# Bringing split operands of attention scores into row layout: DMA from SBUF to SBUF, or through DRAM slots

## The chip, the cores and the metric

The kernel runs on one core of one Trainium2 chip. The metric is the time of one execution in microseconds (us) of device time. The core has five engines that run their own instruction queues in order and wait for each other by semaphores: TensorE (PE; its weight loads are shown as PEld), VectorE (DVE), ScalarE (ACT), GpSimd (POOL) and SyncE (SP), which here only issues DMAs. An instruction at the head of an engine's queue that has to wait holds up everything behind it.

## The reference, cut to what matters

Two layers run one after the other on x of shape (4, 512, 128). The change is in the first layer, whose attention parts are twelve tasks, one for each of four batches in three parts:

```
x = x + 0.5 * ffn(layernorm(x))      # part 0: causal "latent" attention inside, then a mixture of 8 experts
x = x + attn(layernorm(x))           # part 1: full attention
x = x + 0.5 * ffn(layernorm(x))      # part 2: as part 0
# in each part, 16 heads of 8 dimensions:
scores = einsum('bqhd,bkhd->bhqk', q, k) / sqrt(8);  a = softmax(scores);  out = einsum('bhqk,bkhd->bqhd', a, v)
```

The second layer (a chosen-token attention, an additive attention of depth 4, the chosen-token attention again) is not touched.

## The kernel before, in words

**Split operands.** Scores are computed with bf16 operands that together carry f32 precision. q and k (each 128 rows by 512 tokens, f32) are split into three bf16 pieces (`NS` = 3): the leading piece, the leading piece of the remainder, and the rest. A score is the sum over `r` = 0, 1, 2 of products of kA with qA[r]: each of them is a 128-partition tile in which partition 4x + s holds piece s of row x, for four groups of heads (`[P, NG, T]`), and qA[r] pairs the pieces in another rotation. The fourth row of each four (s = 3) is -1 in kA and, in qA[0], half of these rows later hold the (split) maximum of each query's scores, so that the second product comes out as score minus maximum. They must be zero for the first product.

**Making the pieces** (`pieces`, lines 359 to 367): ScalarE writes the leading piece from PSUM (L363), VectorE the remainder (L364, a tile that shares its buffers, tag "v", with the mixture's v of L483), GpSimd the second piece (a cast, L365) and the third (a subtraction, L366). `spread` (L369 to L378) then moves pieces to rows: 12 DMAs of 128 KB from SBUF to SBUF, and from the third task on one more (L374) that sets the maxima's rows of qA[0] back to zero. There are two sets of qA, kA and vA, used by tasks in turn; `fill` (L247) sets the rows that never change, on VectorE, at the start.

**Tasks and units.** `attention` runs a hand-written order over units: a causal task has 10, a full one 16, in all 144, and seven more steps in which only the trailing work runs. In unit n TensorE makes the scores of unit n (`maxima`, L541) with q as the stationary operand, VectorE reduces them to maxima per query and head group, nm (L564 with the causal mask added, L568 without). After a group's last unit, `place_maxima` (L570) is run in the next unit: GpSimd splits the maxima into three pieces (L575 to L578), VectorE transposes them (L580), SP moves them into qA[0] by four DMAs of 4 KB (L584). Some units later (the lag: 5 at the start, 7 from unit 28 on) TensorE makes the scores once more, now transposed and less the maximum (`shifted`, L593), ScalarE takes the exponential (L607), GpSimd masks the diagonal (L613) and TensorE multiplies with the values (L638). PSUM's eight banks are given to products in turn.

**Beside the units** run generators that take one step each half unit: `prepare` of the next task (layernorm statistics on VectorE, the normalised h and, in latent tasks, Y on GpSimd, L330 and L343, transposition and projection on TensorE, the pieces), `place` (which waits until the task two back has left the buffers, then runs `spread` and `values`), `finish`, and the experts' mixture (L274 on TensorE, L479 on ScalarE, L484 on VectorE, L485 on GpSimd), whose gates go through a small DRAM tile (away, L779) and come back broadcast (spread, L470).

**What sets the order.** The program text gives priorities. A scheduler turns it into the order of each engine's instructions by its own model of their times, so an instruction may stand earlier or later in its engine's queue than in the text.

**The start.** Task 0 is prepared ahead of the loop: `fill(0)`, the projections, the pieces, `fill(1)`, constants on GpSimd (L105 to L139 and L259), then `spread`, with its DMAs issued from SP and ScalarE in turn.

Of the kernel before, what the change touches and what calls it, by code (L numbers as in the profile page):

```python
# [8 lines left out]
F32 = mybir.dt.float32  # L9
BF16 = mybir.dt.bfloat16  # L10
AF = mybir.ActivationFunctionType
ALU = mybir.AluOpType
# [30 lines left out]
def tile_macaron(ctx: ExitStack, tc: tile.TileContext, a: dict, out: bass.AP):  # L43
# [52 lines left out]
    causal = const.tile([P, T], F32, name="causal")  # L96
    paired = const.tile([P, P], BF16, name="paired")
    ones = const.tile([P, T], F32, name="ones")
    zeros = const.tile([16, T], BF16, name="zeros")
# [5 lines left out]
    def constants():  # L105


        nc.gpsimd.memset(causal, 0.0)
        make_causal_mask(nc, causal[:, T - P : T], mask_val=NEG)
        nc.gpsimd.memset(ones, 1.0)  # L110
        nc.gpsimd.memset(zeros, 0.0)

    def constants_later():
        nc.gpsimd.tensor_copy(ident_h, ident)
# [119 lines left out]
    def first_layer(opened, picked):  # L234
        with (
# [8 lines left out]
            vAs = [hp.tile([P, NC, NH, 32], F32, name=f"vA{i}") for i in range(2)]  # L244


            def fill(i):  # L247
                for q in qAs[i]:
                    nc.vector.memset(q.rearrange("p g t -> p (g t)").bitcast(F32), 0.0)
                nc.vector.memset(kAs[i], -1.0)  # L250

            fill(0)

            nms = [hp.tile([P, 16], F32, name=f"nm{g}") for g in range(NG)]
            pieces_of = [hp.tile([P, NC, 32], BF16, name=f"mp{g}") for g in range(NG)]
# [27 lines left out]
            class Task:  # L283
# [3 lines left out]
                def __init__(self, part, b, k):  # L287
                    self.part, self.b, self.k = part, b, k
                    self.causal = part != "full"


                    if self.causal:
                        self.units = []
                        for g in range(0, NG, 2):
                            for pieces in ([(g, 3)], [(g, 2), (g, 0)], [(g, 1), (g + 1, 1)], [(g + 1, 2), (g + 1, 0)], [(g + 1, 3)]):
                                at, unit = 0, []
                                for h, c in pieces:
                                    unit.append((h, c, at, (c + 1) * P))
# [6 lines left out]
                    self.qA, self.kA, self.vA = qAs[i], kAs[i], vAs[i]  # L305
                    self.ready = False

                def prepare(self):

                    b = self.b  # L310
                    while self.part == "full" and (0, b) not in mixed:
                        yield
                    h = wp.tile([P, NC, P], F32, name="h")
                    hT = wp.tile([P, T], F32, name="hT", bufs=1)
                    mv = small.tile([P, NC, 2], F32, name="mv")
                    yield from moments_steps(X[:, b], mv)
                    var = mv[:, :, 1]
                    v = small.tile([P, 2 * NC], F32, name="v2")
                    nc.gpsimd.tensor_scalar(v[:, 0:NC], var, 1e-5, None, ALU.add)
                    if self.causal:  # L320


                        nc.gpsimd.tensor_scalar(v[:, NC : 2 * NC], var, 1.0 + 1e-6, 1e-11, ALU.mult, ALU.add)
                    n = 2 * NC if self.causal else NC
                    r = rsqrt(v[:, 0:n], n)
                    yield
                    eng = nc.gpsimd if self.k else nc.vector
                    for c in range(NC):
                        at = n - NC + c
                        eng.tensor_scalar(  # L330
                            h[:, c, :], X[:, b, c, :], mv[:, c, 0:1], r[:, at : at + 1], ALU.subtract, ALU.mult
                        )
                    yield
                    if self.part == "full":
                        nc.gpsimd.tensor_tensor(
                            X[:, b], X[:, b], late["a_bo"].unsqueeze(1).to_broadcast([P, NC, P]), op=ALU.add
                        )
                        nc.scalar.copy(hT, transposed(h))
                        yield
                        wq, wk, self.wv, src = late["a_wq"], late["a_wk"], late["a_wv"], hT  # L340
                    else:
                        for c in range(NC):
                            nc.gpsimd.tensor_scalar(  # L343
                                Y[:, b, c, :], X[:, b, c, :], mv[:, c, 0:1], r[:, c : c + 1], ALU.subtract, ALU.mult
                            )
# [12 lines left out]

                def pieces(self, ps, scale, name):

                    x = [wp.tile([P, T], BF16, name=f"{name}C{s}", bufs=1) for s in range(NS)]
                    rest = wp.tile([P, T], F32, tag="v", name="rest")
                    nc.scalar.activation(x[0], ps, AF.Copy, scale=scale)  # L363
                    nc.vector.scalar_tensor_tensor(rest, ps, scale, x[0], ALU.mult, ALU.subtract)  # L364
                    nc.gpsimd.tensor_copy(x[1], rest)  # L365
                    nc.gpsimd.tensor_tensor(x[2], rest, x[1], op=ALU.subtract)  # L366
                    return x

                def spread(self):  # L369

                    if self.k > 1:
                        nc.sync.dma_start(self.qA[0][NS:P:8], zeros.unsqueeze(1).to_broadcast([16, NG, T]))  # L374
                    moves = [(self.kA[s:P:4], self.kC[s]) for s in range(NS)]
                    moves += [(self.qA[r][s:P:4], self.qC[(s + r) % NS]) for r in range(NS) for s in range(NS)]
                    for i, (to, x) in enumerate(moves):
                        (nc.scalar if self.k == 0 and i % 2 else nc.sync).dma_start(to, x)  # L378

                def values(self):  # L380
                    pv = bank()
# [13 lines left out]
                def place(self):  # L395

                    ago = tasks[self.k - 2] if self.k > 1 else None
                    while not self.ready:
                        yield
                    while ago and now[0] <= ago.start + ago.last[NG - 1] + GAP:  # L400
                        yield
                    self.spread()
                    yield
                    yield
                    while ago and now[0] <= ago.start + len(ago.units) + GAP + LAG:
                        yield
                    self.values()
# [114 lines left out]
            def attention():  # L522
# [47 lines left out]
                def place_maxima(t, g):  # L570

                    m = nms[g].rearrange("p (j c) -> p j c", c=NC)
                    split = pieces_of[g][:, :, 0:16].rearrange("p c (j s) -> p j s c", s=4)
                    rest = wp.tile([P, 4, NC], F32, name="mR")
                    nc.gpsimd.tensor_copy(split[:, :, 0], m)  # L575
                    nc.gpsimd.tensor_tensor(rest, m, split[:, :, 0], op=ALU.subtract)
                    nc.gpsimd.tensor_copy(split[:, :, 1], rest)
                    nc.gpsimd.tensor_tensor(split[:, :, 2], rest, split[:, :, 1], op=ALU.subtract)  # L578
                    mT = wp.tile([P, NC, 32], BF16, name="mT")
                    nc.vector.transpose(mT, pieces_of[g])  # L580
# [828 lines left out]
```

## Time and profile before

| | |
|---|---|
| median of 3 runs | 1445.24 us (1442.93 to 1447.3) |
| the profiled execution: its time, its span | 1445.16 us, 1443.3 us |
| mean granted clock of TensorE | 0.925 |
| DMA, mean over the span | 37 GB/s |

Busy us by stage, from the trace's table of stretches:

| stretch, us | length | PE | DVE | ACT | POOL | PE clock |
|---|---|---|---|---|---|---|
| 0 to 39.5: loads, preparation of task 0 | 39.5 | 7.95 | 14.39 | 4.39 | 32.32 | 0.77 |
| 39.5 to 890: the twelve tasks and the mixtures | 850.5 | 748.68 | 574.95 | 424.02 | 415.38 | 0.91 |
| 890 to 1443: the rest of the mixtures, second layer | 553 | 497.71 | 380.09 | 156.82 | 203.75 | 0.95 |

Products of TensorE overlap, so its busy time is not work at its peak rate; the idle time is what can be read from it. "L541" is line 541 of the kernel. A line of the waits says which instruction was idle, which one released it, for how many us in total, how many times, and the longest. A line of the timeline has the start, the duration, the engine, the line, the operation with what it writes and reads, and in brackets the idle time ahead of it and its releaser. A wait is put down to the last releaser, so behind an in-order engine the instruction named may only have been held up by another one.

### The profile page before, as it was taken

The numbers are of one execution on the slowest core, as the hardware profiler recorded it, in microseconds if no ns is written. First come the engines' busy times: TensorE is split into PE (matmuls) and PEld (weight loads), VectorE is DVE, ScalarE is ACT, GpSimd is POOL, SyncE is SP. The second block draws the span as 40 slices with busy tenths as digits, with TensorE's granted clock in tenths as the row PEclk, the third lists the DMA queues.
The fourth block names the chain that finished last, engine by engine and source line by source line (L and its number), as shares of the span: only waits on it lengthen the run. The fifth ranks groups of instructions, "written<-read, shape, count | busy, mean of one in ns | idle before, by whom it ended". The sixth has DMA issues, their size and how long they took to land. (4 is left out here: it accounts for less than half of the span.)

```text
span 1443.3 us, 32811 instructions
## 1 busy us (share of the span) xinstructions
PE 1254.3 (87%) x12586; PEld 652.5 (45%) x12586; DVE 969.4 (67%) x3321; ACT 585.2 (41%) x1180; POOL 651.5 (45%) x1063
## 2 busy tenths in 40 slices
PE   2787798999998989889769999998969999998698
PEld 0333333343333223334424434346747676766576
DVE  3666676676765767677747754868657676666783
ACT  1244434455555656555425555322313333333122
POOL 8445465666465121214456586561234444443100
PEclk7589799999999999998869999999999999999799
DMA  3201121203012120010103012120100000000000
GB/s 112 71 10 50 37 72 32 77 3 106 4 59 72 35 64 26 25 41 11 49 2 108 26 38 68 39 80 10 29 1 23 16 23 16 1 1 1 1 8 23
DMA packets 66493, 53.07 MB, mean 37 GB/s; under 512 B 24545, under 2 KB 56417, under 8 KB 66337
## 3 DMA queue, kind: packets, MB, share of 16 engines
q1 hardware_dynamic: 63168, 47.86, 11.2%
q10 hardware_dynamic: 3168, 3.12, 0.7%
q8 instruction: 99, 1.62, 0.5%
q14 instruction: 58, 0.47, 0.1%
HBM read 29.45 MB, written 1.18 MB: 21 GB/s over the span
## 5 line engine op out<-in xcount | busy, mean ns | idle before, releaser
L607 ACT ACTIVATE e<-bank 128x512 f32<-128x512 f32 x576 | 312.5, 595 | 303.6 <-PE bank L541 238.7
L541 PE MATMUL bank<-kA,qA 32*128 32x512 bf16 (+3 forms) x2304 | 295.5, 348 | 76.2 <-DVE nm L564 35.4
L564 DVE CUSTOM_DVE_ANT_0 junk<-bank,causal 128x384 f32<-128x384 f32 (+3 forms) x512 | 250.1, 488 | 98.6 <-PE bank L541 58.6
L593 PE MATMUL bank<-qA,kA 32*128 32x512 bf16 (+3 forms) x2304 | 277.8, 342 | 31.7 <-DVE nm L568 17.5
L485 POOL TENSOR_TENSOR hid<-v,spread 128x512 f32<-128x512 f32 x128 | 164.5, 1292 | 96.1 <-DVE v L484 71.2
L638 PE MATMUL sum<-e,vA 128*32 128x256 f32 (+1 forms) x2560 | 195.8, 391 | 9.3 <-POOL e L613 9.3
L593 PEld LDWEIGHTS <-kA 32*128 32x128 bf16 x2304 | 91.1, 95 | 224.3 <-issue 202.7
L568 DVE TENSOR_REDUCE nm<-bank 128x1 f32<-128x512 f32 x256 | 162.5, 682 | 41.2 <-PE bank L541 40.1
L613 POOL TENSOR_SCALAR_AFFINE_SELECT e<-e 128x256 f32<-128x256 f32 x256 | 99.8, 409 | 130.1 <-ACT e L607 129.6
L541 PEld LDWEIGHTS <-qA 32*128 32x128 bf16 x2304 | 105.0, 96 | 95.7 <-issue 82.2
L274 PE MATMUL bank<-tT,sb_f_w 128*32 128x512 f32 x1024 | 140.0, 614 | 2.5 <-DVE v L484 2.3
L274 PE MATMUL sum<-hid,sb_f_w 128*32 128x512 f32 x1024 | 136.0, 598 | 3.0 <-POOL hid L485 2.8
L638 PEld LDWEIGHTS sum<-e,vA 128*32 128x32 f32 x2560 | 65.5, 114 | 142.6 <-issue 125.3
L484 DVE SCALAR_TENSOR_TENSOR v<-th,bank 128x512 f32<-128x512 f32 x128 | 87.4, 684 | 44.9 <-ACT th L479 28.6
L479 ACT ACTIVATE th<-bank 128x512 f32<-128x512 f32 x128 | 76.4, 598 | 54.5 <-PE bank L274 44.3
L156 POOL TENSOR_TENSOR r<-v,mhalf 128x4 f32<-128x4 f32 (+1 forms) x64 | 71.5, 1118 | 5.0
L580 DVE STREAM_TRANSPOSE mT<-mp 128x128 bf16<-128x128 bf16 x48 | 15.0, 312 | 81.2 <-POOL mp L578 80.9
L1283 PE MATMUL bank<-h2T,w 128*128 128x512 f32 x128 | 68.2, 625 | 0.2 <-ACT h2T L1272 0.2
L1289 PE MATMUL bank<-w,hid 128*128 128x128 f32 x512 | 66.9, 280 | 0.1
L1289 PEld LDWEIGHTS bank<-w,hid 128*128 128x128 f32 x512 | 64.0, 197 | 4.5 <-issue 1.0
L1284 ACT ACTIVATE hid<-bank,sb_l_cols 128x512 f32<-128x512 f32 x64 | 44.0, 688 | 39.8 <-PE bank L1283 39.6
L575 POOL CAST mp<-nm 128x16 bf16<-128x16 f32 x48 | 12.3, 256 | 103.2 <-DVE nm L568 74.7
(287 smaller groups left out, 1959.0 us busy)
## 6 DMA issues: line engine op xcount, KB each, us to landing
spread<-away SPq DMA_DIRECT2D x64, 256.0 KB, 3.4
qA<-qC SPq DMA_DIRECT2D x103, 128.0 KB, 2.1
kA<-kC SPq DMA_DIRECT2D x35, 128.0 KB, 2.1
qA<-mT SPq DMA_DIRECT2D x192, 4.0 KB, 1.7
w<-in_l_w_dram SPq DMA_DIRECT2D x8, 256.0 KB, 4.0
sb_m_wqkv<-in_m_wqkv_dram SPq DMA_DIRECT2D x4, 384.0 KB
m_yg<-in_m_trig_dram SPq DMA_DIRECT2D x8, 130.0 KB, 3.2
X<-in_x_dram SPq DMA_DIRECT2D x4, 256.0 KB
```

Source lines behind the costliest of these rows:

```text
L274: nc.tensor.matmul(ps[32 * j : 32 * j + 32, :], lhsT=w[:, 32 * j : 32 * j + 32], rhs=rhs, start=start, stop=stop, skip_group_check=True,)
L479: nc.scalar.activation(th, ph, AF.Tanh, scale=0.5)
L484: nc.vector.scalar_tensor_tensor(v, th, 1.0, ph, ALU.add, ALU.mult)
L485: nc.gpsimd.tensor_tensor(hid, v, self.spread[e], op=ALU.mult)
L541: nc.tensor.matmul(ps[:, at : at + w], lhsT=t.qA[r][rows, g, c * P : (c + 1) * P], rhs=t.kA[rows, g, 0:w], start=r == 0 and k == 0, stop=r ...
L564: nc.vector.tensor_tensor_reduce(junk[:, 0:w], src, causal[:, T - w : T], 1.0, NEG, ALU.add, ALU.max, dst)
L568: nc.vector.tensor_reduce(dst, src, axis=AX.X, op=ALU.max)
L593: nc.tensor.matmul(ps[:, at : at + w], lhsT=t.kA[rows, g, kc * P : (kc + 1) * P], rhs=t.qA[r][rows, g, q0:T], start=r == 0 and k == 0, sto ...
L607: nc.scalar.activation(es[n][:, j, :], ps, AF.Exp)
L613: nc.gpsimd.affine_select(out=e, in_=e, pattern=[[0, 2], [1, P]], compare_op=ALU.is_ge, fill=0.0, base=0, channel_multiplier=-1,)
L638: nc.tensor.matmul(to[32 * j : 32 * j + 32, q0 + lo - at : q0 + hi - at], lhsT=t.vA[:, kc, 4 * j + g, :], rhs=es[n][:, j, lo:hi], start=fresh,
L1289: nc.tensor.matmul(pm[:, c * P : (c + 1) * P], lhsT=hid[:, f, c * P : (c + 1) * P], rhs=w2[:, f, :], start=(f == 0), stop=(f == 3),)
```

## The change

The lines of the changed kernel are given as it has them.

- q and k are split in two steps. `leading` makes the first piece (ScalarE) and the remainder (VectorE, in a buffer of its own, one each for q and k in turn); one half unit later `trailing` makes the other two. For the first task they are VectorE's (a copy L386 and a subtraction L387); for all others the cast is ScalarE's (L383) and the subtraction GpSimd's (L384).
- From the second task on the pieces go through DRAM. `away` writes them to slots, each 128 rows of 1 KB (four DMAs: 384, 256, 128 and 384 KB); `back` reads kA and each of the three qA in one DMA of 512 KB, in which each partition takes 4 KB from the slot of its piece. Slots with zeros and with -1 are written once (`fixed_rows`), so that the rows of the maxima come back as zeros with the rest. Two sets of slots are used in turn. The clearing DMA of L374 and the filling of the second set of buffers are gone.
- The first task keeps moves from SBUF to SBUF (`first_rows`), with the pieces rotated the other way.
- `place_maxima` only splits; the transposition and the DMAs (`move_maxima`) are put on the list of the next unit.
- The causal mask is kept in bf16. The zeros of 16 rows that GpSimd set are gone; VectorE sets a tile of zeros and one of -1 at the start.

```diff
-            def fill(i):
-                for q in qAs[i]:
-                    nc.vector.memset(q.rearrange("p g t -> p (g t)").bitcast(F32), 0.0)
-                nc.vector.memset(kAs[i], -1.0)
-
-            fill(0)
+            for q in qAs[0]:
+                nc.vector.memset(q.rearrange("p g t -> p (g t)").bitcast(F32), 0.0)
+            nc.vector.memset(kAs[0], -1.0)
+            zeros = wp.tile([P, 2 * T], BF16, tag="aT", bufs=1, name="zeros")[:, 0:T]
+            nc.vector.memset(zeros.bitcast(F32), 0.0)
+            minus = wp.tile([P, 2 * T], BF16, tag="junk", bufs=1, name="minus")[:, 0:T]
+            nc.vector.memset(minus, -1.0)
+            qds = [dp.tile([10, P, T], BF16, name=f"qd{i}", bufs=1) for i in range(2)]
+            kds = [dp.tile([NS + 1, P, T], BF16, name=f"kd{i}", bufs=1) for i in range(2)]
+            def fixed_rows():
+                for i in range(2):
+                    nc.sync.dma_start(qds[i][9], zeros)
+                    nc.sync.dma_start(kds[i][NS], minus)
...
-                    self.qC = self.pieces(ps, HD**-0.5, "q")
+                    self.qC, rest = self.leading(ps, HD**-0.5, "q")
+                    yield
+                    self.trailing(self.qC, rest)
+                    yield
                     yield
                     ps = bank()
                     by_columns(ps, wk, src)
-                    self.kC = self.pieces(ps, 1.0, "k")
+                    self.kC, rest = self.leading(ps, 1.0, "k")
+                    yield
+                    self.trailing(self.kC, rest)
                     self.ready = True
...
+                def leading(self, ps, scale, name):
+                    x = wp.tile([P, NS, T], BF16, name=f"{name}C", bufs=1)
+                    rest = wp.tile([P, T], F32, name="rest", bufs=1)
+                    nc.scalar.activation(x[:, 0], ps, AF.Copy, scale=scale)
+                    nc.vector.scalar_tensor_tensor(rest, ps, scale, x[:, 0], ALU.mult, ALU.subtract)
+                    return x, rest
+                def trailing(self, x, rest):
+                    if self.k:
+                        nc.scalar.copy(x[:, 1], rest)
+                        nc.gpsimd.tensor_tensor(x[:, 2], rest, x[:, 1], op=ALU.subtract)
+                    else:
+                        nc.vector.tensor_copy(x[:, 1], rest)
+                        nc.vector.tensor_tensor(x[:, 2], rest, x[:, 1], ALU.subtract)
...
+                def away(self):
+                    def put(slots, x):
+                        nc.sync.dma_start(slots.rearrange("s p t -> p s t"), x)
+                    put(self.qd[6:9], self.qC)
+                    put(self.qd[0:6:3], self.qC[:, 1:3])
+                    put(self.qd[5:6], self.qC[:, 0:1])
+                    put(self.kd[0:NS], self.kC)
+                def back(self):
+                    def rows(slots):
+                        return slots.rearrange("s (x g) t -> x s g t", g=NG)
+                    nc.sync.dma_start(self.kA, rows(self.kd))
+                    for r in range(NS):
+                        nc.sync.dma_start(self.qA[r], rows(self.qd[(6, 3, 0)[r] : 10 : r + 1]))
...
                     while not self.ready:
                         yield
+                    yield
+                    self.away()
+                    yield
                     while ago and now[0] <= ago.start + ago.last[NG - 1] + GAP:
                         yield
-                    self.spread()
+                    self.back()
...
                     nc.gpsimd.tensor_tensor(split[:, :, 2], rest, split[:, :, 1], op=ALU.subtract)
+                    later.append(lambda: move_maxima(t, g))
+                def move_maxima(t, g):
                     mT = wp.tile([P, NC, 32], BF16, name="mT")
                     nc.vector.transpose(mT, pieces_of[g])
...
-            fill(1)
...
-            tasks[0].spread()
+            tasks[0].first_rows()
+            fixed_rows()
```

More of the change, by code (lines that the diff above doesn't have):

```diff
@@ L95, in tile_macaron @@
     ident_h = const.tile([P, P], BF16, name="ident_h")
-    causal = const.tile([P, T], F32, name="causal")
+    causal = const.tile([P, T], BF16, name="causal")
     paired = const.tile([P, P], BF16, name="paired")
     ones = const.tile([P, T], F32, name="ones")
-    zeros = const.tile([16, T], BF16, name="zeros")
     before = const.tile([P, NE, NE], F32, name="before")
@@ L110, in constants @@
         nc.gpsimd.memset(ones, 1.0)
-        nc.gpsimd.memset(zeros, 0.0)
     def constants_later():
@@ L305, in __init__ @@
                     self.qA, self.kA, self.vA = qAs[i], kAs[i], vAs[i]
+                    self.qd, self.kd = qds[i], kds[i]
                     self.ready = False
@@ L355, in prepare @@
                     by_columns(ps, wk, src)
-                    self.kC = self.pieces(ps, 1.0, "k")
+                    self.kC, rest = self.leading(ps, 1.0, "k")
+                    yield
+                    self.trailing(self.kC, rest)
                     self.ready = True
[L359 to L376, printed above, removed]
-                    for i, (to, x) in enumerate(moves):
-                        (nc.scalar if self.k == 0 and i % 2 else nc.sync).dma_start(to, x)
+                def leading(self, ps, scale, name):
[4 more added lines that the diff above has]
+                    return x, rest
@@ new lines, in trailing, with first_rows @@
+                def trailing(self, x, rest):
[5 more added lines that the diff above has]
+                        nc.vector.tensor_tensor(x[:, 2], rest, x[:, 1], ALU.subtract)
+                def first_rows(self):
+                    moves = [(self.kA[s:P:4], self.kC[:, s]) for s in range(NS)]
+                    moves += [(self.qA[r][s:P:4], self.qC[:, (s - r) % NS]) for r in range(NS) for s in range(NS)]
+                    for i, (to, x) in enumerate(moves):
+                        (nc.scalar if i % 2 else nc.sync).dma_start(to, x)
```

## The prediction

> **What bounds the kernel now.** The page's busy shares come first: TensorE 87%, VectorE 67%, ScalarE 41%, GpSimd 45%. TensorE is the engine to keep fed, and the stretch tables say where it is not. From 0 to 39.5 us it is busy 7.95 us; from 39.5 to 890 us (first layer) 748.7 of 850.5 us; after that 497.7 of 553 us. The change touches the first two stretches only, so the list of waits is read for them. Its columns are the waiting instruction, what released it, total us, times, longest.
>
> ```profile
> PE bank L541 <- DMA kA<-kC: 21.8, 1, 21.8
> DVE mT L580 <- POOL mp L578: 80.9, 45, 10.1
> PE bank L541 <- DVE nm L564: 35.4, 23, 7.4
> PE bank L593 <- DVE nm L568: 17.5, 3, 7.9
> ```
>
> The reader is to see one long wait (TensorE on the first task's kA) and one repeated chain: the transposition of the maxima waits for GpSimd, VectorE's reductions wait behind it, and TensorE waits for their banks. The timeline at the start (start, duration, engine, line) shows who makes kA late:
>
> ```profile
> 16.57 0.66 DVE L364 SCALAR_TENSOR_TENSOR rest<-bank,kC 128x512 f32<-128x512 f32 x1
> ...
> 34.80 0.61 POOL L365 CAST kC<-rest 128x512 bf16<-128x512 f32 x1
> 35.40 0.81 POOL L330 TENSOR_SCALAR h<-X,mv,r 128x128 f32<-128x128 f32 x1
> 36.18 1.15 POOL L366 TENSOR_TENSOR kC<-rest,kC 128x512 bf16<-128x512 f32 x1
> 37.32 2.35 POOL L330 TENSOR_SCALAR h<-X,mv,r 128x128 f32<-128x128 f32 x3
> ...
> 39.56 3.48 PE L541 MATMUL bank<-kA,qA 32*128 32x512 bf16 x38 [21.76 <-DMA kA<-kC]
> 39.66 3.14 POOL L343 TENSOR_SCALAR Y<-X,mv,r 128x128 f32<-128x128 f32 x4
> ...
> 52.67 0.25 POOL L575 CAST mp<-nm 128x16 bf16<-128x16 f32 x1 [9.88 <-DVE nm L564]
> ...
> 53.94 0.31 DVE L580 STREAM_TRANSPOSE mT<-mp 128x128 bf16<-128x128 bf16 x1 [0.87 <-POOL mp L578]
> ```
>
> VectorE has the remainder of k at 17.2, but GpSimd, full of constants and the preparation of tasks 1 and 2, splits it only at 37.3. Kernel start, then, hangs on GpSimd's queue.
>
> **Step 1, first task's split on VectorE.** Added to VectorE's start: memsets of zeros (a quarter of the 0.91 us row) and minus (a quarter of the 1.76 us row), with gaps 1.1 us; removed from it: the second filling, 3 x 0.91 + 1.76 us, which lay beside waits. All that hangs on the first statistics moves 1.1 us later. ScalarE's copy of q then ends at 15.9 (14.15 + 0.60 + 1.1). VectorE follows with remainder 0.66, copy, subtraction, for q and k. The trace has no such copy; nearest are a VectorE operation with one f32 SBUF input at 0.55 us (L985) and a copy out of PSUM at 0.68 (L959). I take 0.55. The subtraction is as the two-input rows, 0.66. Two times 1.9 us and small gaps: kC complete at 19.7. From GpSimd's last split to the first product it was 39.56 - 37.33 = 2.2 us; so the first product comes at 21.9, 17.6 us earlier.
>
> It doesn't all arrive. Group 0 of the first task took 52.67 - 39.56 = 13.1 us, set by VectorE's reductions, so its maxima would be done at 35.0. The next step is GpSimd's split of them, and in the built order of the changed kernel GpSimd still has the preparation of tasks 1 and 2 ahead of it. That run ended at 42.80 and had no gap after 9.6; it loses four operations (0.62 + 1.15 + 0.61 + 1.15 = 3.53) and the memset of zeros (0.52), and starts 1.1 later: 39.85. The split takes 1.27, so the transposition comes at 41.1 instead of 53.94: **12.8 us gained**, with the gate handed from kA to GpSimd's backlog. Bounds: 17.6 if the backlog isn't in the way. If GpSimd's traffic slows the four new VectorE operations by 1.0 us each (one two-input row, L722, took 1.70 instead of 0.66), the maxima are done at 39.0, still under the 39.85.
>
> [...] In the trace L722's eight runs are 0.66 us but for one of 1.70, which started during a GpSimd multiplication. [...]
>
> **Step 2, maxima split one unit ahead.** If it worked as worded, the repeated chain would go. I read the order of instructions in both built programs: the scheduler places them, and in it the transposition stands where it stood, right behind the last reduction of its group (47 of 48 within four VectorE instructions), with GpSimd's h and Y ahead of the split as before. The six longest stalls of TensorE that follow a transposition (7.44 at 146.9, 2.20 at 182.1, 5.53 at 256.0, 7.85 at 470.2, 4.80 at 534.9, 4.80 at 600.0) have the same sequence of work ahead of them. Taken: 0. Bounds: 0 to 32.6 gained, the sum of the six.
>
> One place changes for the worse: ahead of the stall at 470 the two statistics that start h and Y stand four reductions later than before (behind 12 and 14 of a group's 16, not 8 and 10). Reductions come in pairs every 1.45 us, so GpSimd's 14 us chain starts **2.9 us** later against the group's end. Bounds 0 to 2.9.
>
> **Step 3, remainders.** k's remainder now stands later than right behind the transposition. TensorE's waits for remainders (L364) are 6.9 + 5.5 + 1.9 = 14.3 us in this stretch; the bank then waited for is that of the next reduction, 0.55 us instead of 0.69, behind the same transposition. I take **3 us gained**; bounds 0 and 14.3. For tasks 1 to 11 the cast goes from GpSimd (0.61) to ScalarE (0.60 by its f32-to-bf16 row L363), 22 times. GpSimd gains little: it waited 41.0 us for these remainders. ScalarE's cast waits for VectorE, and exponentials queue behind it: 0.8 us in the usual case (the remainder ends at most 0.83 after ScalarE's copy in 14 of the 22, up to 3.4 in the others) plus 0.60. Taken: 0, since ScalarE waits 238.7 us for L541's banks and already carries copies of 0.59 us between exponentials; bounds 0 and 22 x 1.4 = 31 us lost.
>
> **Step 4, DRAM slots.** Per task 13 issues of SP (12 moves of 128 KB, one of 64 KB) become 8: 1.15 MB out in four, 2 MB back in four. Issue is 0.6 us each; landing is 2.3 us for 256 KB out (out_dram), 3.4 to 4.0 us for 256 KB in (spread, w). No row shows 512 KB alone; the load phase moved 244 to 339 GB/s, so 2 MB take 6 to 8.5 us and some 3 us to land. The old moves took 8 us and 2.1: no later. Both wait for the same last product two tasks back; three units remain, some 16 us (850.5 us over 151 units are 5.6 each). The maxima's small moves queue behind them, but at lag 7 have four units. Two tight places: task 4, whose k is split after its predecessor's third group (out and back end at about 289 in before's time, needed at 289.7), and group 1 of the first task (57 to 58, needed at 57.3). I take **1 us lost**; bounds 0 and 3 us at each of 11 tasks, 33. The nearest row for a short way out and back is away, 16 KB: issued at 173.06, its first reader at 174.55. [...]
>
> **Step 5, causal in bf16.** A 512-wide reduction takes 0.686 us with the mask and 0.682 without: nothing to gain, 0.
>
> **Sum**: -12.8 + 0 + 2.9 - 3 + 0 + 1 + 0 = -11.9 us. The profiled execution took 1445.16 us (span 1443.3 and 1.9 around it), the median is 1445.24: **1433 us**.
>
> **Rivals.** (a) The transposition does stop waiting: up to 32.6 us more, 1401. For it: the program text; against it: the built order. (b) The change doesn't do what it says on time: the first 12.8 us are given back in changed stalls (three or four more shifts like the 2.9 us of step 2, since every statistic in the built order has moved a little), 1441 to 1449. (c) **Slower**: ScalarE's casts block it. Each of 22 holds exponentials 1.4 us; banks go back late and TensorE stops. Full price 31 us: 1433 + 31 = 1464. It decides from 16.2 / 22 = 0.74 us paid per cast (the sum reaches +0.3%, 4.3 us). For it: ScalarE is in order, two exponentials (1.09 us) fill most of a 1.45 us half unit in the full attention; against it: only 2.6 us of TensorE's waits in this kernel are on a ScalarE copy (oU, 7 times, longest 0.6).
>
> **Numbers.** Forecast 1424 to 1441: 0.62. Beyond it, (a) in part or whole or the full 17.6 us: 0.13. (b) 0.12. (c), with late read-backs, 0.13. What a measurement of this kernel can tell from no change is 0.3%, so faster means below 1440.9: 0.75; the same 0.12; slower 0.13. The range leaves out most of (a) and of (c): 1417 to 1447.
>
> **What would show it.** First product near 22; first transposition near 41 with some 5 us of wait on GpSimd's mp; 75 to 85 us on that wait in all; the 7 to 10 us stalls of the first and second part still there; no TensorE wait on kA or qA above 1 us later than the start; ScalarE waits for rest near 18 us, with TensorE's waits on ScalarE under 8. A first product after 28, a short mT wait in total, or TensorE waiting on qds or kds would prove me wrong.

## The result, and the profile after

The changed kernel is slower: 1459.47 us median (1455.5 to 1461.17, 4 runs) against 1444.09 us (1442.02 to 1447.3), a ratio of 1.0101 with a 95% interval of 1.0071 to 1.0131. The forecast was 1433 us. The profiled execution has a span of 1459.0 us and a clock of 0.92; the time went in the second stage, the first layer: from 39.5 to 890 us TensorE is busy for 733.70 us, not 748.68.

The start did what was forecast. The timeline of the changed kernel:

```profile
15.02 3.54 POOL L270 MEMSET vA<- 128x2048 f32 x2
...
16.32 3.54 DVE L386 CAST qC<-rest 128x512 bf16<-128x512 f32 x1
...
21.41 0.52 DVE L386 CAST kC<-rest 128x512 bf16<-128x512 f32 x1
...
25.16 1.03 PE L583 MATMUL bank<-kA,qA 32*128 32x512 bf16 x9 [7.37 <-DMA kA<-kC]
...
40.35 0.25 POOL L617 CAST mp<-nm 128x16 bf16<-128x16 f32 x1
...
41.61 0.31 DVE L625 STREAM_TRANSPOSE mT<-mp 128x128 bf16<-128x128 bf16 x1 [1.55 <-POOL mp L620]
```

The first product comes at 25.16, not 39.56, the first transposition at 41.61, not 53.94: 12.33 us gained. To see where they went again, line up the 48 transpositions of the two kernels, one for each group of each task, and follow the difference (the expectations below call this the ledger). It is -12.3 us at the first, still -10.5 as the fifth task begins (318.5 before), +3.7 two groups later, +11.4 at the third group of the sixth task, and +11 to +18 from there on. So some 28 us were lost, and the difference made 22 of them in three groups.

Such a step says that a group ended later, not that TensorE stood still for it. In the last of the three (8.3 us) TensorE's stall is 4.1 us longer than before (11.91 against 7.85); the trace also has 32 more of the mixtures' products between these two transpositions than before, work that had only moved. Nor is idle time the whole loss: against the kernel with the first task's split alone (the first experiment; span 1430.4 us), the changed kernel's span is 28.6 us longer with the same 12586 products. TensorE's idle time grew by 16.3 us (176.2 to 192.5) and its busy time by 12.3 (1254.2 to 1266.5). The last section shows what may be one reason for the second: behind each stall of over 4 us in this stage the granted clock was 0.50 for some us, and behind the one near 470 a pair of products took 0.60 to 0.63 us, not 0.38 or 0.39.

The waits of the first 890 us (waiting instruction, releaser, total us, times, longest):

```profile
DVE mT L625 <- POOL mp L620: 102.6, 45, 12.4
...
PE bank L583 <- DVE nm L606: 25.5, 22, 5.5
PE bank L638 <- DVE nm L610: 23.5, 6, 11.9
...
ACT kC L383 <- DVE rest L377: 20.9, 10, 10.6
...
PE bank L638 <- DVE rest L377: 11.9, 6, 8.8
PE bank L583 <- ACT e L652: 10.9, 14, 1.5
...
PE bank L583 <- DMA kA<-kC: 7.4, 1, 7.4
```

Against before: the transposition's wait for GpSimd did not go but grew (80.9 to 102.6). One row is new: TensorE behind exponentials, 14 times some 0.8 us. And the waits of the second product behind a remainder (before 5.5 us, 2.6 at most) now hold one of 8.8 us. That one is the group with the first large loss. Read its timeline from the bottom up:

```profile
318.63 3.52 SPq L403 DMA_DIRECT2D qd<-qC  x3
...
322.28 0.48 SPq L824 DMA_DIRECT2D away<-gT  x1
...
324.81 1.62 SPq L417 DMA_DIRECT2D qA<-qd  x2
...
326.54 1.95 SPq L512 DMA_DIRECT2D spread<-away  x4
...
333.68 1.26 POOL L527 TENSOR_TENSOR hid<-v,spread 128x512 f32<-128x512 f32 x1 [12.10 <-DMA spread<-away]
...
336.14 0.31 DVE L625 STREAM_TRANSPOSE mT<-mp 128x128 bf16<-128x128 bf16 x1 [10.23 <-POOL mp L620]
...
337.06 0.62 ACT L383 CAST kC<-rest 128x512 bf16<-128x512 f32 x1 [10.57 <-DVE rest L377]
337.08 0.58 PE L638 MATMUL bank<-qA,kA 32*128 32x512 bf16 x1 [8.75 <-DVE rest L377]
```

The gates leave at 322.28. Behind them on SP's queue stand two read-backs of the slots, which hold SP until 326.4; only then go the gates' broadcast loads, and these land 7 us later, behind 1 MB of read-back. GpSimd, whose next instruction needs them, stood 12.10 us. In the kernel before it was 2.26 at this place:

```profile
331.43 1.27 POOL L485 TENSOR_TENSOR hid<-v,spread 128x512 f32<-128x512 f32 x1 [2.26 <-DMA spread<-away]
```

The maxima's split stands behind it on GpSimd, the transposition behind that, k's remainder behind the transposition on VectorE, the cast behind the remainder on ScalarE, and TensorE behind all of them.

### The profile page after: what moved, and what is told of

Read it like the earlier page. It is cut to its first block, busy times and chain, and to the rows that moved or that the text cites. A ratio compares the mean times of both kernels' runs of the same rounds, so it can differ in the third digit from the quotient of the medians.

```text
span 1459.0 us, 32733 instructions
## 1 busy us (share of the span) xinstructions
PE 1266.5 (87%) x12586; PEld 655.4 (45%) x12586; DVE 972.1 (67%) x3323; ACT 596.5 (41%) x1202; POOL 632.4 (43%) x1036
## 5 line engine op out<-in xcount | busy, mean ns | idle before, releaser
L638 PE MATMUL bank<-qA,kA 32*128 32x512 bf16 (+3 forms) x2304 | 281.5, 347 | 55.4 <-DVE nm L610 23.5
L683 PE MATMUL sum<-e,vA 128*32 128x256 f32 (+1 forms) x2560 | 194.7, 388 | 10.5 <-POOL e L658 8.6
L638 PEld LDWEIGHTS <-kA 32*128 32x128 bf16 x2304 | 93.1, 96 | 233.7 <-issue 207.7
L281 PE MATMUL bank<-tT,sb_f_w 128*32 128x512 f32 x1024 | 144.6, 620 | 3.1 <-DVE v L526 2.3
L625 DVE STREAM_TRANSPOSE mT<-mp 128x128 bf16<-128x128 bf16 x48 | 14.9, 310 | 102.9 <-POOL mp L620 102.6
L1226 PE MATMUL bank<-wa,hT 128*128 128x385 f32 x128 | 56.7, 543 | 1.4 <-ACT hT L1219 1.4
```

Of the source, the lines that this page charges most:

```text
L281: nc.tensor.matmul(ps[32 * j : 32 * j + 32, :], lhsT=w[:, 32 * j : 32 * j + 32], rhs=rhs, start=start, stop=stop, skip_group_check=True,)
L638: nc.tensor.matmul(ps[:, at : at + w], lhsT=t.kA[rows, g, kc * P : (kc + 1) * P], rhs=t.qA[r][rows, g, q0:T], start=r == 0 and k == 0, sto ...
L683: nc.tensor.matmul(to[32 * j : 32 * j + 32, q0 + lo - at : q0 + hi - at], lhsT=t.vA[:, kc, 4 * j + g, :], rhs=es[n][:, j, lo:hi], start=fresh,
```

## The experiments

First theory: the slots' transfers hold up urgent small ones. Their DMAs are called puts (`away`, to DRAM) and read-backs (`back`). Rivals: ScalarE's casts block it; the added pauses (the new `yield`s, each half a unit long) shift the order of the work. The change has these three parts besides the first task's split, and all eight combinations were run. Each time is compared with the kernel before on the same chip (1444.2 to 1445.4 us in the five sets).

**The first task's split alone**, in the kernel before:

```diff
-                    nc.gpsimd.tensor_copy(x[1], rest)
-                    nc.gpsimd.tensor_tensor(x[2], rest, x[1], op=ALU.subtract)
+                    eng = nc.gpsimd if self.k else nc.vector
+                    eng.tensor_copy(x[1], rest)
+                    eng.tensor_tensor(x[2], rest, x[1], op=ALU.subtract)
```

> The kernel before with one edit: the first task's two later pieces of q and k are made on VectorE, not on GpSimd. In the changed kernel the first transposition began 12.33 us earlier than before, and the ledger of the 48 transpositions stands 27 us worse at 700 us. If those 27 us belong to other parts of the change, the 12.3 us stay: 1432 us. If the later stretches give back whatever the start gains, 1440 to 1444.

Measured: 1431.02 us, ratio 0.9905 (0.9887 to 0.9923). The 12.3 us of the first transposition are there at every later one (9.7 to 13.4). Nothing gives them back; the loss belongs to the other parts.

**One part undone each time.** The slots, with the moves from SBUF to SBUF in their place (the main lines):

```diff
-                    put(self.qd[6:9], self.qC)
...
-                    nc.sync.dma_start(self.kA, rows(self.kd))
+                    moves = [(self.kA[s:P:4], self.kC[:, s]) for s in range(NS)]
+                    moves += [(self.qA[r][s:P:4], self.qC[:, (s - r) % NS]) for r in range(NS) for s in range(NS)]
+                    for to, x in moves:
+                        nc.sync.dma_start(to, x)
```

> The changed kernel with the twelve moves from SBUF to SBUF in the place of the slots (the read-back's place), all else as changed. Theory of the slots: the puts and read-backs on SP's queue hold up the gates' broadcast loads (12.10 us of wait at 333.7, where the gates had left at 322.3), and the two steps of 6.35 and 7.89 us in the fifth task go with them: 1445. Theory of the casts on ScalarE, and theory of the shifted steps of the preparation: within 3 us of the changed kernel, 1457 to 1462.

Measured: 1442.84 us, 0.9991 (0.9975 to 1.0008): 16.6 us less than the changed kernel. The rows of zeros come from a small DRAM tile, and the second set of buffers is filled by VectorE as before. The casts, back on GpSimd:

```diff
-                        nc.scalar.copy(x[:, 1], rest)
+                        nc.gpsimd.tensor_copy(x[:, 1], rest)
```

> The changed kernel with the 22 casts of the second piece back on GpSimd, nothing else. Theory of the casts: the 14 half-unit stalls of TensorE behind ScalarE, 10.9 us in all, go, and the 11.9 us that TensorE stood behind the remainder go in part: 1446 to 1449. Theory of the slots and of the shifted steps: 1456 to 1462, as GpSimd gets 22 casts of about 0.6 us more.

Measured: 1447.22 us, 1.0009 (0.9994 to 1.0025): 12.3 less. TensorE's waits behind exponentials fall from 10.9 to 1.2 us on the first product; GpSimd's wait for the gates' loads at 330 is still there, 12.39 us. The maxima's two steps, in one again:

```diff
-                    later.append(lambda: move_maxima(t, g))
-                def move_maxima(t, g):
```

> The changed kernel with the maxima's splitting and transposition in one step again. VectorE's built order differs in one transposition of 48, GpSimd's and ScalarE's not at all; on SP the moves of the transposed maxima change places with the gates' loads. All three theories: 1456 to 1462; a gain of over 5 us would say that the places on SP's queue decide and that the split of the step is what moved them.

Measured: 1455.57 us, 1.0068 (1.005 to 1.0087), lower than the range written down, but the interval overlaps that of the changed kernel: not told apart. Of this part there is nothing large to find. The pauses, taken out:

```diff
                     self.qC, rest = self.leading(ps, HD**-0.5, "q")
-                    yield
                     self.trailing(self.qC, rest)
-                    yield
                     yield
...
                     self.kC, rest = self.leading(ps, 1.0, "k")
-                    yield
                     self.trailing(self.kC, rest)
...
-                    yield
                     self.away()
-                    yield
```

> The changed kernel with the added pauses of the preparation and of the placing taken out again: remainder's split in the same step as its product, k in the step after q, puts and read-back without pauses between; slots and ScalarE's casts stay. Theory that the shifted steps cost: where the slots and the casts were undone, the fifth and sixth task's third groups still fell back by 7.7 and 8.3 us, so these go: 1443 to 1449. Theory that slots (16.6) and casts (12.3) make up the whole loss: 1456 to 1462.

Measured: 1441.87 us, 0.9966 (0.9951 to 0.9981): 17.6 less. Three parts that seem to cost 16.6, 12.3 and 17.6 us cannot all do so: the whole loss against the split alone is 28. So the parts were also run alone, with the same edits combined. Pauses alone:

> The changed kernel without slots and with the casts on GpSimd; the added pauses stay. If the two prices add: 1459.5 - 16.6 - 12.3 = 1430.6. If both sat in one stall (the 10.23 us at 336): 1440 to 1443.

Measured: 1433.95 us, 0.9918 (0.9894 to 0.9943). None of the three:

> Without slots, casts on GpSimd, without the added pauses: of the change only the first task's split on VectorE, the remainder's own buffer, the maxima's two steps and the bf16 mask are left. As the first task's split alone, if those three are worth nothing: 1428 to 1434. If the remainder's own buffer brings something, below 1425.

Measured: 1432.87 us, 0.9923 (0.9902 to 0.9943): as the split alone. Own remainder buffer, bf16 mask and the maxima's two steps are worth nothing that can be measured. Slots alone:

> As the kernel with nothing left but the first task's split, yet with the slots in DRAM: casts on GpSimd, no added pauses. If the slots cost by themselves, as in the pair that left them out (16.6): 1444 to 1449. If they cost only where the pauses bring their transfers ahead of the gates' loads: 1429 to 1435.

Measured: 1432.09 us, 0.9916 (0.9895 to 0.9937). The slots alone cost nothing, and my first theory as I had put it falls. Casts alone:

> As the kernel with nothing left but the first task's split (1432.9), yet with the 22 casts on ScalarE; no slots, no added pauses. If the casts cost by themselves, as in the pair that differs in them beside the slots (1441.9 against 1432.1): 1441 to 1445. If, like slots and pauses, they cost only in company: 1431 to 1435.

Measured: 1444.01 us, 0.9991 (0.9978 to 1.0004). All together, medians in us:

| | slots: no | slots: yes |
|---|---|---|
| no casts on ScalarE, no pauses | 1432.9 | 1432.1 |
| pauses | 1434.0 | 1447.2 |
| casts | 1444.0 | 1441.9 |
| casts and pauses | 1442.8 | 1459.5 |

The casts cost 9 to 12 us in every company. Slots and pauses cost nothing singly (-0.8 and +1.1) and 14 together. For the pauses that nothing is a balance: in the profiles, the transposition of the fifth task's second group comes 21.7 us earlier than in the kernel before with pauses alone, and 11.8 with none of the three; the last transposition, 11.9 and 11.8. Two questions follow: why together, and by what the casts cost.

**Why slots and pauses together.** With the pauses q is ready before the gates of the task three back, so the scheduler puts q's puts and read-backs ahead of the gates' loads on SP; without them the loads come first. Only that order is changed here, in the kernel with slots and pauses (1447.2):

```diff
-                    self.back()
+                    if self.k == 5:
+                        while not loads_of:
+                            yield
+                        with tc.issue_after(loads_of[0]):
+                            self.back()
+                    else:
+                        self.back()
```

> The changed kernel with the casts on GpSimd (1447.2) and one more edit: the sixth task's read-backs are put on SP's queue behind the first four of the gates' loads, which they stand among or ahead of. On every other engine the built order is the same, on SP two read-backs move. If the loads' place behind the read-backs makes the 11 us wait for the maxima near 333: the wait falls to about 4, and 1440 to 1442. If it is the amount that the slots move, whatever the order: 1446 to 1449.

Measured: 1443.07 us, 0.9982 (0.9967 to 0.9997), 4.1 less. The place, for comparison with the one above:

```profile
320.65 0.34 SPq L830 DMA_DIRECT2D away<-gT  x1
...
322.97 1.95 SPq L518 DMA_DIRECT2D spread<-away  x4
...
325.04 1.24 SPq L417 DMA_DIRECT2D qA<-qd  x2
...
326.32 1.26 POOL L533 TENSOR_TENSOR hid<-v,spread 128x512 f32<-128x512 f32 x1 [6.51 <-DMA spread<-away]
```

Loads first, and GpSimd waits 6.51, not 12.39. The amount moved is the same. The other losses of this pair are at 109 and 172. Of the first, the DMA table of the changed kernel from 95 to 112 us shows the reason (KB each, median us from issue to landing):

```profile
qA<-qd SPq DMA_DIRECT2D x3, 512.0 KB, 8.0
...
qA<-mT SPq DMA_DIRECT2D x4, 4.0 KB, 7.0
```

Moves of 4 KB that land in 1.8 us by the median of the whole run took 7.0 here, issued behind three of 512 KB. TensorE stood 3.07 us for one. Both places were put in order as well:

```diff
+                    elif self.k == 2:
+                        while (1, 1) not in sent:
+                            yield
+                        with tc.issue_after(sent[1, 1]):
+                            self.back()
...
+                    if self.k == 3 and 0 in sent:
+                        with tc.issue_after(sent[0]):
+                            put(self.kd[0:NS], self.kC)
...
+                    while self.k == 3 and 0 not in sent:
+                        yield
```

> The kernel with the sixth task's read-backs behind the gates' loads (1443.1), and two more such moves on SP's queue: the third task's read-backs behind the moves of the second task's second group of maxima, where TensorE stood 2.66 us for such a move at 108.7; and the fourth task's put of k behind the first gates' loads. VectorE, GpSimd and ScalarE keep their built order. If the order on SP's queue is the whole price of slots and pauses together: 2.7 there, and some 5 at 172 where the maxima waited 5.70 us and not 1.7: 1434 to 1437. If the amount moved is: 1441 to 1445.

Measured: 1437.42 us, 0.9942 (0.9925 to 0.9958). Three changes of order on one queue, with the orders of VectorE, GpSimd and ScalarE untouched, take 9.8 of the 13.3 us by which slots and pauses (1447.2) stood above pauses alone (1434.0). The last 3.4 us lie within the intervals; whether anything is left there is open. The amount moved was the same in these three kernels, so it is not the amount that made these 9.8.

**By what the casts cost.** Each cast takes 618 ns, and ScalarE waits for its remainder first. One experiment adds the work without the wait:

```diff
+                        nc.scalar.copy(x[:, 2], x[:, 0])
                         nc.gpsimd.tensor_copy(x[:, 1], rest)
```

> The kernel with nothing left but the first task's split (1432.9, casts on GpSimd), and 22 copies on ScalarE of the size of the casts, each right behind the activation that made its source, so that it waits for nothing; what they write is overwritten by the third piece. The casts on ScalarE cost 11 us. If what costs is ScalarE's 0.6 us of work: 1442 to 1445. If it is ScalarE's standing still for VectorE's remainder: 1432 to 1435.

Measured: 1433.54 us, 0.9927 (0.9907 to 0.9947). 22 copies of 618 ns each cost nothing. The other keeps the casts (no slots, pauses; 1442.8) and takes the wait away:

```diff
-                        nc.scalar.copy(x[:, 1], rest)
+                        with tc.issue_after(last_exp[0]) if last_exp[0] else ExitStack():
+                            nc.scalar.copy(x[:, 1], rest)
```

> The kernel without slots (added pauses, casts on ScalarE; 1442.8), with each cast put behind the two exponentials that come next in ScalarE's queue; there it stood right behind the activation of the first piece, and waited 26 us in all for VectorE's remainder. VectorE's order hardly changes. If the price of the casts (8.9 us against the same kernel with them on GpSimd, 1434.0) is that wait: ScalarE's waits for the remainder fall below 10 us, the stalls of TensorE behind exponentials go, and 1434 to 1437. If it is the work: 1441 to 1445.

Measured: 1432.16 us, 0.9916 (0.9899 to 0.9932): the whole price is gone. The waits with the casts right behind their activation, 40 to 890 us:

```profile
ACT kC L377 <- DVE rest L371: 13.2, 10, 4.0
ACT qC L377 <- DVE rest L371: 13.2, 11, 3.0
...
PE bank L571 <- ACT e L640: 11.0, 14, 1.5
```

and with the casts two exponentials later:

```profile
ACT qC L378 <- DVE rest L371: 3.3, 2, 1.7
ACT kC L378 <- DVE rest L371: 3.2, 3, 2.8
...
PE bank L572 <- ACT e L641: 1.5, 1, 1.5
```

ScalarE's 26.4 us of waiting became 6.5, and TensorE's 11.0 behind exponentials 1.5. So the wait is the price, by these two runs; the way from it to TensorE is shown only in part. With the casts alone (no pauses) the same row has 4.8 us, against 0.4 in the kernel with none of the three, for the same price of 11. And in the profiles of either pair TensorE's idle time differs by 4.1 us; the rest stands in its busy time, in products that took longer (7.5 and 9.6 us). What made them longer there was not found.

**The stall near 470.** The pauses put the statistics of the next two preparations later; GpSimd's chain behind them sets the transposition. First the kernel with slots alone, then the changed one:

```profile
436.29 0.23 POOL L327 TENSOR_SCALAR v<-mv 128x4 f32<-128x4 f32 x1 [9.90 <-DVE mv L171]
...
452.07 0.31 DVE L620 STREAM_TRANSPOSE mT<-mp 128x128 bf16<-128x128 bf16 x1 [9.36 <-POOL mp L615]
...
453.01 0.61 PE L633 MATMUL bank<-qA,kA 32*128 32x512 bf16 x2 [7.85 <-DVE nm L605]
```

```profile
464.93 0.23 POOL L327 TENSOR_SCALAR v<-mv 128x4 f32<-128x4 f32 x1 [12.21 <-DVE mv L171]
...
480.63 0.31 DVE L625 STREAM_TRANSPOSE mT<-mp 128x128 bf16<-128x128 bf16 x1 [12.39 <-POOL mp L620]
...
481.57 0.61 PE L638 MATMUL bank<-qA,kA 32*128 32x512 bf16 x2 [11.91 <-DVE nm L610]
```

From v to the transposition it is 15.8 and 15.7 us in both: GpSimd's r, h, X, r, h and Y stand ahead of the split of the maxima. The stall grew by 4.1 us. With pauses alone it is 11.98, so the slots and the casts have no part in it. Since the chain is GpSimd's, part of it was moved, in the kernel with slots alone:

```diff
-                            nc.gpsimd.tensor_scalar(
+                            nc.vector.tensor_scalar(
                                 Y[:, b, c, :], X[:, b, c, :], mv[:, c, 0:1], r[:, c : c + 1], ALU.subtract, ALU.mult
```

> The kernel with the slots alone (casts on GpSimd, no added pauses; 1432.1), and the normalized rows Y (20 instructions, 797 ns each on GpSimd) on VectorE. GpSimd's backlog ahead of the maxima at 450, 15.7 us long, gets 3.1 shorter, others of latent tasks as well: 1426 to 1430 if the backlog is what the stalls hang on. If VectorE's own time decides: 20 x 386 ns = 8 us more there, 1434 to 1440.

Measured: 1421.07 us, 0.9832 (0.9818 to 0.9847), the fastest of all, 11 us under the same kernel with Y on GpSimd. TensorE's stall at this place:

```profile
446.30 1.16 DVE L351 TENSOR_SCALAR Y<-X,mv,r 128x128 f32<-128x128 f32 x4 [5.32 <-POOL r L154]
...
448.12 0.58 PE L633 MATMUL bank<-qA,kA 32*128 32x512 bf16 x1 [5.56 <-DVE nm L605]
```

It is 5.56, not 7.85, and now VectorE stands for r in the middle of its reductions; the four rows of Y take 1.16 us there and took 3.14 on GpSimd. The transposition's waits for GpSimd fall to 51.8 us in all (78.8 with Y on GpSimd). Between 100 and 890 us TensorE's stalls of over 4 us are four, 26.3 us in all, and not six of 38.4. Four more tried how far this goes: h on VectorE too (`eng = nc.vector`), the second piece's casts on VectorE too, Y on VectorE with pauses and without slots, and Y on VectorE with neither.

> As the one with Y on VectorE, and h there too (44 more instructions in the part up to 890 us). If GpSimd's backlog decides: the 7.85 us stall at 453 goes nearly whole and the two of 4.80 in part: 1418 to 1426. If VectorE, which would stand behind the root r on GpSimd (1.0 to 1.7 us each time, more behind a backlog), is blocked instead: 1436 or more.

Measured: 1430.53 us, 0.9898 (0.9882 to 0.9913), a miss. VectorE stands 24.0 us in 9 waits of h for r. Against Y alone 4.7 us are lost by the second group of the sixth task; what takes them there was not followed further.

> The kernel with Y on VectorE (1421.1), and the casts of the second piece on VectorE too: 22 x 0.62 = 13.6 us less for GpSimd, and no hand-over between remainder and cast; VectorE gets 22 x 0.52 = 11 us more (the first task's second cast). If GpSimd's backlog still sets the stalls: 1414 to 1419. If VectorE is now as late as GpSimd: 1421 to 1427.

Measured: 1425.57 us, 0.987 (0.985 to 0.989): no gain over Y alone, a loss of 4.5.

> The kernel without slots, with the added pauses and the casts on GpSimd (1434.0), and Y on VectorE. If Y's place brings what it brought beside the slots (11.0): 1423. If the remainder stalls that the pauses remove (3.3 and 3.5 us, still there with Y on VectorE) come on top: 1416 to 1420.

Measured: 1423.02 us, 0.9849 (0.983 to 0.9868): Y brings 10.9 us without slots and with the pauses as well; the remainder stalls do not come on top.

> The fastest kernel so far (slots, no added pauses, casts on GpSimd, Y on VectorE; 1421.1) with moves from SBUF to SBUF in the place of the slots. If the slots bring nothing by themselves, as without Y's move (1432.1 against 1432.9): 1419 to 1424. If they bring something once GpSimd is less late: 1425 or more.

Measured: 1427.98 us, 0.9894 (0.9874 to 0.9914): 7 us above the kernel with slots, against the first of the two expectations. They are there from the start: VectorE fills the second set of buffers (0.91, 0.91 and 1.76 us) ahead of q's remainder, the first transposition is at 45.89 and not 43.15, the second task's second group at 107.95 and not 101.59. With slots that filling isn't needed.

## Why the prediction was wrong

- **Step 1** (first task on VectorE, -12.8): right, -12.33 at the first transposition, and -14.0 us alone between the medians of the first experiment's set. GpSimd's backlog set the moment (split at 40.35, forecast 39.85). The first product came at 25.16, not at 21.9, near the 25.9 of the bound with four operations slowed by 1.0 us each (21.9 + 4.0); it was one cast that took 3.54 us, so the nearness is luck. The backlog covered it, as forecast, but by 0.3 us and not by 4.9 (39.85 less 35.0): VectorE had the last maximum at 40.06. The wait on mp was 1.55, not 5, for this reason.
- **Step 2** (maxima, 0; statistics near 470, +2.9): right in kind. The transposition's waits grew, the stalls stayed, and the stall at 470 grew by 4.1. Rival (a) is refuted: 102.6 us of wait. The cause was put down to the split of the maxima; the runs show that it is the pauses, as it is 7.85 or 7.86 in the kernels without them (before, slots alone, none of the three, slots and casts).
- **Step 3, remainders** (-3): with the pauses, without slots and casts, TensorE's waits for remainders are 8.2 us, without any of the three 14.2: a gain of about 6 that does not reach the time (pauses alone: +1.1). The longer stall at 470 takes back 4.1 of it; the rest was not followed.
- **Step 3, casts** (0; GpSimd's waits for the remainders were 41.0 us for q alone and 47.3 with k's, and nothing hangs on it): this term was mis-sized; it is 9 to 12 us, 0.5 us a cast. Rival (c) had its mechanism, and the reason for setting it to nothing was the error: that ScalarE has 238.7 us of idle time and carries copies of 0.59 us already. That is true of its work, and the copies without a wait cost nothing. But the price of an instruction in an in-order queue that waits for another engine is not its work. Alone it brings the time from 1432.9 to 1444.0, no change from before; rival (c)'s 31 us were too much, and its row, TensorE behind exponentials, shows only a part of the price.
- **Step 4** (slots, +1): alone right (-0.8), but 14.3 us with the pauses of step 3. Beside the casts, this is the step that failed, at its words "no later": it asked when kA and qA arrive, and TensorE hardly ever waited for those (0.3 us after the start). It did not ask who stands behind the puts and read-backs on SP: the gates' loads and the maxima's moves. Its words "the maxima's small moves queue behind them, but at lag 7 have four units" miss the start, where the lag is 5 and a move took 7.0 us. The built order showed both; I had read VectorE's and GpSimd's order and not SP's.
- **The sum**: the steps were priced one by one and added. Two of them had one price together that neither had alone; the built order of the whole change is where it could be seen. No step asked for the granted clock behind a stall (0.50). Rival (b), gains given back because the order moved, named the kind; its 8 to 16 us were too few.
- **Step 5** (mask, 0): no run disagrees; it is part of the 1432.9.

## What to carry to other kernels

When a change moves transfers, read the order on the issuing queue as closely as that of the compute engines, and ask of each large transfer which small, urgent one stands behind it: here 10 us hung on three places in SP's order. Price an instruction that is moved to a less busy engine by what it waits for, not by its length: 22 copies without a wait cost nothing, 22 with one cost 9 to 12 us, and two exponentials' distance made them free again. And where a repeated wait names one engine, look what else that engine does just ahead of it: thirty-two small instructions taken off GpSimd brought 11 us, to 1421 us, about as much as the first task's split.

## What the runs showed of the hardware

The first task's cast of q took 3.54 us on VectorE and that of k, of the same shape, 0.52. Beside the first, GpSimd ran six memsets without a gap, the two of 128x2048 from 15.02 to 18.56 and four small ones to 19.57; the cast ended at 19.86, 0.29 us after them. In the kernel with Y on VectorE and no slots, where the casts (at 20.75 and 22.87) came after these memsets (done at 16.45), both took 0.40. So the cast beside the memsets was 7 times as long as its fellow; that the memsets held it up is the author's estimate from these rows, and by what way they would no run shows.

A small transfer's time to landing depended on what stood ahead of it on the same queue: 4 KB took 1.8 us by the median and 7.0 behind three of 512 KB, and 1.8 by the median at that place (90 to 112 us) in the kernel with all three places in order; a gates' load of 256 KB took 3.0 us at best and 7.2 behind read-backs. It was not always paid for: the load of 7.2 us was issued at 779.51, and GpSimd's last wait for such a load in the first 890 us ended at 776.59. Whether another queue would have let the small ones pass was not tried.

The granted clock fell at TensorE's long stalls. Every one of over 4 us between 100 and 890 us, six in the kernel before and eight in the changed one, was followed by a stretch at a clock of 0.50, which began during the stall or at most 0.6 us behind it and lasted 3.6 to 7.7 us beyond it. Here is the stall at 470 in the kernel before, the stretch ahead of it and the one behind, and then the stretch behind the same stall in the changed kernel (length; busy us and instructions of TensorE, its weight loads, VectorE, ScalarE, GpSimd; clock, DMA share, GB/s):

```profile
450.00:462.30 12.30, 12.18 (x152) 5.67 (x145) 9.56 (x28) 8.34 (x17) 8.32 (x11) 1.00 0.01 1
462.30:470.20 7.90, 0.05 (x5) 0.06 (x4) 0.97 (x3) 0.37 (x1) 6.66 (x12) 0.68 0.00 0
470.20:475.40 5.20, 5.20 (x40) 1.05 (x39) 3.69 (x7) 1.85 (x4) 0.00 (x0) 0.50 0.27 53
...
481.60:487.80 6.20, 6.20 (x51) 1.57 (x51) 4.29 (x7) 2.17 (x4) 0.00 (x0) 0.50 0.33 87
```

Products took longer at that clock: in the changed kernel a pair of L638 with 512 columns took 0.38 or 0.39 us just ahead of the stall (466.04 to 468.52), 0.60 to 0.63 behind it (481.57 to 487.36, at clock 0.50), and 0.38 or 0.39 again from 487.79 on, at 1.00. How much of the 12.3 us of longer products this makes was not measured.
